# Depthwise convolution of a scan layer as stacks of three shifted rows on four column quarters of TensorE

## The chip, the cores and the metric

The kernel runs on one NeuronCore of a Trainium2 chip. The metric is the time of one execution on the device, in microseconds (us); lower is better. TensorE (PE) does matrix products and transposes, VectorE (DVE) and ScalarE (ACT) element-wise work, GpSimd (POOL) element-wise work on SBUF alone, and SyncE (SP) issues the DMAs. Matmuls write into PSUM, eight banks of 512 float32 columns on 128 partitions.

## What is computed

Two layers on eight images of 56 x 56 positions and 192 channels, all in float32. The first layer normalizes groups, makes queries, keys and values by depthwise 3 x 3 convolutions and 1 x 1 projections, attends with three heads and adds the result to its input. The second layer, in which the change lies, is a two-dimensional selective scan over 384 inner channels. Cut to its core:

```python
xz = jnp.einsum('bhwc,oc->bhwo', x, in_proj_w)
xa, z = jnp.split(xz, 2, axis=-1)
xc = conv_general_dilated(xa, conv_w, (1, 1), 'SAME', feature_group_count=Din) + conv_b
xc = silu(xc)
...
h = exp(d_l * A) * h + d_l * B_l * u_l     # scan over 3136 positions, 16 states
y = sum(h * C_l, axis=-1)
...
```

The convolution is depthwise: each of the 384 channels has its own nine weights, and no channel mixes with another.

## The kernel before

**Tiling.** The 3136 positions of an image are cut into 7 chunks of `T = 448` (`RPC = 8` rows of 56); the 384 channels into `NJ = 3` blocks of 128. A scan step is one state `n` of 16 for one chunk of one direction: 4 directions x 7 chunks x 16 states = 448 steps for an image, 3584 in all. A step takes one product of step size and B row on GpSimd (L1119), three exponentials on ScalarE (L1133) and three scans on VectorE (L1150). To multiply by C and sum the states, TensorE turns the state tile `h` (L1196), ScalarE scales it while it leaves PSUM (L1212), and TensorE turns it back into an accumulating PSUM tile `y` (L1230). For three or four of the 16 states (`BY_POOL`), GpSimd multiplies by C instead (L1248, L1252), and TensorE adds the result with the identity (L1267). Seven buffers `h` are shared by all of this, and five buffers `bb` hold the B rows that DMAs bring.

**Stages.** `front(b)` is everything for image `b` up to the convolved channels: loading, first layer, in-projection, depthwise convolution, Silu. `x_proj` makes step sizes and the rows B and C; `finish` normalizes, gates and projects. The front of image 0 runs ahead of any scan. The front of image `b + 1` runs beside the scan of image `b`; the last image's scan has only a finish beside it.

**What sets the order.** The program is recorded in an order made by hand-written planning code (`Sched`). Each piece of work is a generator that yields `(engine, cost, cells read, cells written)`; the planner keeps a clock for each engine, gives the next instruction to the stage with the earliest time less its rank, and so fixes the order in which each engine's instructions stand. On the chip, engines run their instructions in that order and wait on semaphores. The costs are formulas in the code, `t_mm(n) = n * 0.00171` for a matmul among them. Two rules matter here. `pace` lets the front spend its planned TensorE time in proportion to the scan's progress: beside a given scan step stands a given share of the front's whole TensorE cost. And `keep_busy` puts filler matmuls (L1363) where TensorE's planned clock has a gap. DMAs all go through SyncE's one queue, in planned order.

**The convolution.** In `project`, for each channel block `j`, seven in-projections (two matmuls each, L853) go to PSUM, and `xa_out` (L818) evicts each with its bias into a full-image tile `xa` in SBUF. Then, for each of the seven chunks, `conv_rows` (L452) makes nine matmuls, one for each tap: the stationary operand is a 128 x 128 diagonal matrix of that tap's weights (`dg`, loaded from `dgx_d`), the moving operand the image shifted by the tap, with the rows and columns that fall off the image left out. `xv_out` (L824) evicts the sum, and `stored` applies Silu, and writes the image out once in row order and once in column order. `xa` and `xv` have one buffer each. During scans the front has one PSUM bank at a time (`share("bank1", 1)`); in the head it has eight.

The three lines that carry the convolution:

```python
for t in TAPS:
    yield PE, t_mm(T), xa.c[max(c - 1, 0):c + 2] + dg.c, pcv.c if t == 8 else []
    conv_rows(pcv.ap[:, :T].rearrange("p (h w) -> p h w", w=HW), dg.ap[:, t], ...)
```

Of the kernel before, what the change touches and what calls it, by code (L numbers as in the profile page):

```python
# [8 lines left out]
F32 = mybir.dt.float32  # L9
AF = mybir.ActivationFunctionType  # L10
ALU = mybir.AluOpType
# [6 lines left out]
B, HW, C = 8, 56, 192  # L18
L = HW * HW
CP = 96  # L20
NB = C // CP
T = 448
RPC = T // HW
NCH = L // T
# [10 lines left out]
NJ = DIN // 128  # L35
# [18 lines left out]
PE, ACT, DVE, POOL, SP = range(5)  # L54
# [10 lines left out]
def t_mm(n):  # L65
    return n * 0.00171
# [10 lines left out]
def t_dve(n):  # L77
    return 0.07 + n * 0.00105
# [195 lines left out]
def kernel(  # L274
# [24 lines left out]
    nc = tc.nc  # L299
# [13 lines left out]
    ident = const.tile([128, 128], F32, name="ident")  # L313
# [3 lines left out]
    zeros = fill("zeros", [128, 128], 0.0)  # L317
# [60 lines left out]
    dconst = ctx.enter_context(tc.tile_pool(name="dconst", bufs=1, space=DRAM))  # L378
# [2 lines left out]

    dgq_d = dconst.tile([CP, NB, 9, CP], F32, name="dgq_d")
    dgkv_d = dconst.tile([CP, NB, 9, CP], F32, name="dgkv_d")
    dgx_d = dconst.tile([128, NJ, 9, 128], F32, name="dgx_d")
    with tc.tile_pool(name="taps", bufs=2) as taps:
        for dst, src, p, nb in ((dgq_d, dw_q, CP, NB), (dgkv_d, dw_kv, CP, NB), (dgx_d, conv_w, 128, NJ)):
            w = taps.tile([p, nb, 9], F32, name="w")
            nc.sync.dma_start(w, src.rearrange("(b p) t -> p b t", p=p))
            for bl in range(nb):
                d = taps.tile([p, 9, p], F32, name="d")  # L390
                for t in range(9):
                    nc.vector.tensor_scalar(d[:, t], ident[:p, :p], w[:, bl, t:t + 1], None, ALU.mult)
                nc.sync.dma_start(dst[:, bl], d)


    keep = ctx.enter_context(tc.tile_pool(name="keep", bufs=1))
# [9 lines left out]
    sc = Sched()  # L406
    banks = [None]

    def bank():
        return banks[0]  # L410
# [34 lines left out]
    def conv_rows(out, lhs, img, row0, rows, t):  # L445


        dy, dx = divmod(t, 3)
        lo, hi = max(row0 + dy - 1, 0), min(row0 + dy - 1 + rows, HW)
        o0, o1 = lo - (row0 + dy - 1), hi - (row0 + dy - 1)  # L450
        a, b = max(0, 1 - dx), min(HW, HW + 1 - dx)
        nc.tensor.matmul(out[:, o0:o1, a:b], lhs, img(lo, hi)[:, :, a + dx - 1:b + dx - 1],  # L452
                         start=(t == TAPS[0]), stop=(t == TAPS[-1]))
# [19 lines left out]
    def front(b):  # L473
# [307 lines left out]
        k_nb = Cell()  # L781
        with tc.tile_pool(name=f"fw_{b}", bufs=1) as fw, tc.tile_pool(name=f"fi_{b}", bufs=2) as pool:
            fi, fv = Rings(pool, 2), Rings(fw, 1)
            wx = fw.tile([CP, NB, DIN], F32, name="wx")
            wz = fw.tile([CP, NB, DIN], F32, name="wz")
            k_w = [Cell(), Cell()]
            yield from scaled_weights(wx, k_w[0], 0, rstd1, k_gn1)
            yield from scaled_weights(wz, k_w[1], 1, rstd1, k_gn1)
            pn = yield bank()
            for i, w in enumerate((wx, wz)):  # L790
                yield PE, 1.2, [k_w[i], k_gn1], pn.c if i else []
                for j in range(NJ):
# [13 lines left out]

            tiles, ends = {}, []

            def load_x1():
                for j in range(NJ):  # L810
                    for c in range(NCH):
                        xt = yield fi("xt2", [CP, NB, T])
                        yield from dma([k_x1[c]], xt.c, 5.0, xt.ap, x1d[:, :, c * T:(c + 1) * T])
                        tiles[j, c] = xt

            def xa_out(pin, xa, j, c):
                yield DVE, t_dve(T), pin.c + [k_nb], [xa.c[c]]
                nc.vector.tensor_scalar(xa.ap[:, c * RPC:(c + 1) * RPC].rearrange("p h w -> p (h w)"), pin.ap[:, :T],  # L818
                                        nbias[:, j:j + 1], None, ALU.add)
                pin.free()  # L820

            def xv_out(pcv, xv, j, c):
                yield ACT, t_act(T), pcv.c, [xv.c[c]]
                nc.scalar.activation(xv.ap[:, c * T:(c + 1) * T], pcv.ap[:, :T], AF.Identity, bias=cb[:, j])  # L824
                pcv.free()

            def stored(xv, j):
                k1 = Cell()
                yield ACT, t_act(L) + 2.6, xv.c, [k1]
                nc.scalar.activation(xv.ap, xv.ap, AF.Silu)  # L830
                nc.scalar.preload_act_table_set(EXP_LN)
                yield from dma([k1], [k_xcs[0][c][j] for c in range(NCH)], 6.6, xcs[0][:, j], xv.ap)
                for c in range(NCH):
                    xw = yield fi("xw", [128, RPC, HW])
                    yield ACT, t_act(T), [k1], xw.c
                    nc.scalar.copy(xw.ap, xv.ap.rearrange("p (h w) -> p w h", w=HW)[:, c * RPC:(c + 1) * RPC])
                    if c == NCH - 1:
                        xv.free()
                    yield from dma(xw.c, [k_xcs[1][c][j]], 3.0, xcs[1][:, j, c * T:(c + 1) * T],
                                   xw.ap.rearrange("p a b -> p (a b)"), [xw])  # L840

            def project():
                for j in range(NJ):
                    dg = yield fi("dg", [128, 9, 128], bufs=1)
                    yield from dma([], dg.c, 5.0, dg.ap, dgx_d[:, j])
                    xa = yield fv("xa", [128, HW, HW], parts=NCH)
                    for c in range(NCH):
                        yield lambda: (j, c) in tiles
                        xt = tiles[j, c]
                        pin = yield bank()  # L850
                        yield PE, 2 * t_mm(T), xt.c + [k_w[0]], pin.c
                        for bl in range(NB):
                            nc.tensor.matmul(pin.ap[:, :T], wx[:, bl, j * 128:(j + 1) * 128], xt.ap[:, bl],  # L853
                                             start=(bl == 0), stop=(bl == NB - 1))
                        xt.free()
                        sc.spawn(xa_out(pin, xa, j, c))
                    xv = yield fv("xv", [128, L], parts=NCH)
                    for c in range(NCH):
                        pcv = yield bank()
                        for t in TAPS:  # L860
                            yield PE, t_mm(T), xa.c[max(c - 1, 0):c + 2] + dg.c, pcv.c if t == 8 else []
                            conv_rows(pcv.ap[:, :T].rearrange("p (h w) -> p h w", w=HW), dg.ap[:, t],
                                      lambda lo, hi: xa.ap[:, lo:hi], c * RPC, RPC, t)
                        if c == NCH - 1:
                            xa.free()
                            dg.free()
                        sc.spawn(xv_out(pcv, xv, j, c))
                    ends.append(sc.spawn(stored(xv, j)))

            lx = sc.spawn(load_x1())  # L870
            pj = sc.spawn(project())
            yield from sc.join([lx, pj])
            yield from sc.join(ends)

    def x_proj(b, todo):
# [559 lines left out]
```

## Time and profile before

| what | value |
|---|---|
| median of three runs | 18,205.7 us (18,203.6 to 18,205.72) |
| the profiled execution | 18,215.8 us, its span 18,214.1 us |
| mean granted TensorE clock | 0.982 |
| first scan starts at | 814 us |
| scans of images 1 to 6 | about 2,200 us each |
| scan of image 7, with no front beside it | 16,360 to 18,160 us |
| DMA traffic | 2,159 MB, mean 119 GB/s, 39.7% of the DMA engines' time |

The profile comes from one execution that was profiled. Busy shares are of the whole span. A group's row gives line, engine, operation, output and inputs, shapes and count, then busy time, mean length of one in nanoseconds, and the engine's idle time just before, with what ended it. TensorE's matmuls are pipelined, so the recorded length of one is longer than the distance between two starts; a float32 matmul appears as two records, each with its own weight load (PEld). A view by windows gives the busy time of each engine in stretches of the span.

### The profile page before, as it was taken

To read this page: it belongs to the slowest core of one execution; us is meant where nothing else is said; L and a number is where in the kernel's file an instruction comes from. 1 tells how busy PE (TensorE), PEld (TensorE's weight loads), DVE (VectorE), ACT (ScalarE), POOL (GpSimd) and SP (SyncE) were. 2 spreads that over 40 slices of the span, in tenths; PEclk is the share of its full clock that TensorE was granted. 3 is DMA by queue.
4 is the path that set the end of the run, shared out by engine and by line. 5 is a ranking of instruction groups with operands and counts; after the bars stand their busy time and mean duration, and the time that the engine had idled before them with its cause. 6 is when DMAs were issued, how large, how long until landed. Compare 5 with 4: busy or idle time off the path is not lost. (4 is left out here: it accounts for less than half of the span.)

```text
span 18214.1 us, 279960 instructions
## 1 busy us (share of the span) xinstructions
PE 16706.4 (92%) x99872; PEld 11743.7 (64%) x99872; DVE 14151.5 (78%) x17811; ACT 14223.5 (78%) x25030; POOL 15560.9 (85%) x5200
## 2 busy tenths in 40 slices
PE   8799999999999999999999999999999999999998
PEld 4466666666666666666666666666666666667776
DVE  2277777788878788787887877878878788888998
ACT  2377788687877878778787887878888787888888
POOL 0288899888998889888898889988899888999998
PEclk9899999999999999999999999999999999999999
DMA  1353345433453334533344334553345433453332
GB/s 54 115 161 90 94 142 158 119 90 107 140 170 97 94 112 139 163 99 95 116 147 152 99 92 120 150 150 95 96 127 155 135 93 95 135 153 120 97 96 78
DMA packets 1363539, 2158.99 MB, mean 119 GB/s; under 512 B 176112, under 2 KB 1346016, under 8 KB 1359072
## 3 DMA queue, kind: packets, MB, share of 16 engines
q1 hardware_dynamic: 1362144, 2141.09, 39.7%
q8 instruction: 791, 12.96, 0.3%
q14 instruction: 604, 4.95, 0.1%
HBM read 1649.41 MB, written 491.21 MB: 118 GB/s over the span
## 5 line engine op out<-in xcount | busy, mean ns | idle before, releaser
L1150 DVE TENSOR_TENSOR_SCAN h<-da,newc,h 128x448 f32<-128x448 f32 x9216 | 10104.9, 1137 | 1970.7 <-ACT da L1133 1380.5
L1119 POOL TENSOR_TENSOR h<-du_s,bb 128x1344 f32<-128x1344 f32 x3584 | 10825.3, 3053 | 927.5 <-PE ht L1196 816.2
L1133 ACT ACTIVATE da<-dl_s,acoef 128x448 f32<-128x448 f32 x10752 | 6750.8, 638 | 1756.9 <-DVE h L1150 1705.7
L1212 ACT ACTIVATE g<-ht,ct_s 112x384 f32<-112x384 f32 x10864 | 5847.5, 575 | 936.1 <-PE ht L1196 771.3
L1230 PEld LDWEIGHTS y<-ident,g 112*128 112x128 f32 x32592 | 3564.4, 142 | 2902.0 <-ACT g L1212 1954.4
L1230 PE MATMUL y<-ident,g 112*128 112x112 f32 x32592 | 4799.3, 268 | 654.3 <-ACT g L1212 530.1
L1196 PE MATMUL ht<-ident,h 128*112 128x128 f32 x32592 | 4944.2, 276 | 122.5 <-ACT g L1212 46.6
L1196 PEld LDWEIGHTS ht<-ident,h 128*112 128x112 f32 x32592 | 3683.2, 135 | 482.7 <-DVE h L1150 147.3
L1150 DVE TENSOR_TENSOR_SCAN h<-da,h 128x448 f32<-128x448 f32 x1536 | 1607.5, 1078 | 459.6 <-ACT da L1133 410.9
L1248 POOL TENSOR_TENSOR yp<-h,cb 128x1344 f32<-128x1344 f32 x448 | 1366.3, 3050 | 407.6 <-PE y L1267 173.7
L1248 POOL TENSOR_TENSOR h<-h,cb 128x1344 f32<-128x1344 f32 x420 | 1281.6, 3051 | 292.0 <-issue 171.9
L1363 PE MATMUL y<-zeros 128*128 128x64 f32 x11648 | 1486.5, 271 | 0.0
L1363 PEld LDWEIGHTS y<-zeros 128*128 128x128 f32 x11648 | 1444.5, 194 | 50.2 <-issue 50.2
L920 POOL TENSOR_TENSOR v<-v,xs 128x1344 f32<-128x1344 f32 x224 | 677.3, 3043 | 824.7 <-DMA dl<-v 773.6
L1252 POOL TENSOR_TENSOR yp<-yp,h 128x1344 f32<-128x1344 f32 x420 | 1280.1, 3048 | 32.2
L452 PE MATMUL bank<-xa,dg 128*128 128x440 f32 (+2 forms) x3024 | 1237.1, 535 | 24.2 <-ACT xv L824 19.2
L1267 PE MATMUL y<-yp,ident 128*128 128x448 f32 x2688 | 1223.4, 546 | 10.7 <-POOL yp L1252 10.2
L756 PE MATMUL bank<-qT,kT 128*112 128x448 f32 x2352 | 1074.5, 573 | 138.6 <-DVE oT L719 82.9
L765 PE MATMUL bank<-pT,vt 112*128 112x448 f32 x2352 | 999.9, 543 | 12.4 <-ACT g L1212 6.6
L706 ACT ACTIVATE pT<-bank,nsh 112x448 f32<-112x448 f32 x1176 | 740.1, 632 | 207.2 <-PE bank L756 167.1
L452 PE MATMUL bank<-band,dgq 96*96 96x440 f32 (+3 forms) x2016 | 806.4, 532 | 10.7 <-ACT hq L582 7.7
L452 PEld LDWEIGHTS bank<-xa,dg 128*128 128x128 f32 x3024 | 525.8, 191 | 364.6 <-issue 289.9
(146 smaller groups left out, 11082.0 us busy)
## 6 DMA issues: line engine op xcount, KB each, us to landing
bb<-rows SPq DMA_DIRECT2D x3584, 224.0 KB, 3.4
cb<-rows SPq DMA_DIRECT2D x868, 224.0 KB, 3.7
dl<-v SPq DMA_DIRECT2D x224, 672.0 KB, 5.0
du<-v SPq DMA_DIRECT2D x224, 672.0 KB, 6.1
du_s<-du SPq DMA_DIRECT2D x224, 672.0 KB, 4.5
dl_s<-dl SPq DMA_DIRECT2D x224, 672.0 KB, 4.6
xt<-x1d SPq DMA_DIRECT2D x224, 336.0 KB, 4.6
xch<-xv SPq DMA_DIRECT2D x24, 1568.0 KB, 7.3
```

The lines of the kernel that those rows point to most:

```text
L452: nc.tensor.matmul(out[:, o0:o1, a:b], lhs, img(lo, hi)[:, :, a + dx - 1:b + dx - 1], start=(t == TAPS[0]), stop=(t == TAPS[-1]))
L756: nc.tensor.matmul(ps.ap[:TP, :T], kts[h][:, kb * TP:(kb + 1) * TP], qh.ap, start=True, stop=True)
L1119: nc.gpsimd.tensor_tensor(h.ap, du.ap, bb.ap.unsqueeze(1).to_broadcast([128, NJ, T]), ALU.mult)
L1133: nc.scalar.activation(da.ap[:, :T], dl.ap[:, j], AF.Exp, scale=acoef[:, k * NJ + j, n:n + 1])
L1150: nc.vector.tensor_tensor_scan(h.ap[:, j, rev], da.ap[:, 0:T][:, rev], h.ap[:, j, rev], news[i - 1].ap[:, j, n:n + 1] if ci else 0.0, ALU. ...
L1196: nc.tensor.transpose(ht.ap[:TP, j * 128:(j + 1) * 128], h.ap[:, j, s * TP:(s + 1) * TP], ident)
L1212: nc.scalar.activation(g.ap, ht.ap[:TP, :DIN], AF.Copy, scale=ct.ap[:, s, n:n + 1])
L1230: nc.tensor.matmul(y["t"].ap[:, j, s * TP:(s + 1) * TP], g.ap[:, j * 128:(j + 1) * 128], ident[:TP, :TP], is_transpose=True, start=(n == 0 ...
L1248: nc.gpsimd.tensor_tensor(to.ap, h.ap, cbr.ap.unsqueeze(1).to_broadcast([128, NJ, T]), ALU.mult)
L1252: nc.gpsimd.tensor_tensor(yp.ap, yp.ap, h.ap, ALU.add)
L1267: nc.tensor.matmul(y["t"].ap[:, j, :T], ident, yp.ap[:, j], start=False, stop=(y["left"][j] == 0))
L1363: nc.tensor.matmul(ybanks[:, 0, T:T + FILL], zeros, zeros[:, :FILL], start=False, stop=False)
```

## The change

The depthwise convolution of the second layer is laid out in another way. The evicted in-projection goes, with a zero column on each side, into a small tile `padded` and from there to a DRAM image `xpd` of 58 x 58 positions whose first and last rows are zeroed once at setup. For each channel block and chunk, three DMAs read it back into a tile `stack`: partitions 32 dy to 32 dy + 31 hold 32 channels of the rows shifted by `dy`, with four groups of channels side by side in the free dimension. A matmul with 96 rows then sums three vertical taps of 32 channels; its stationary operand is three diagonals of 32 x 32 on top of each other. Four such matmuls, one for each group of channels, write to output partitions 0, 32, 64 and 96 of the same bank; three of these fours, one for each horizontal shift `dx`, make the convolution of a chunk. The planner counts one `t_mm(T)` for each four. In-projection, loading of stacks and convolution become three stages of their own, where they were one loop before.

```diff
-    dgx_d = dconst.tile([128, NJ, 9, 128], F32, name="dgx_d")
+    dgx_d = dconst.tile([96, NJ, 4, 3, 32], F32, name="dgx_d")
+    xpd = [dconst.tile([128, NJ, HW + 2, HW + 2], F32, name=f"xpd{i}") for i in range(2)]
+    for t in xpd:
+        for row in (0, HW + 1):
+            nc.sync.dma_start(t[:, :, row], zeros[:, :HW + 2].unsqueeze(1).to_broadcast([128, NJ, HW + 2]))
...
+        for j in range(NJ):
+            d = taps.tile([96, 4, 3, 32], F32, name="d3")
+            for g in range(4):
+                for dx in range(3):
+                    nc.vector.tensor_scalar(d[:, g, dx], id3, w3[:, j, g, dx:dx + 1], None, ALU.mult)
+            nc.sync.dma_start(dgx_d[:, j], d)
...
-            def xa_out(pin, xa, j, c):
-                yield DVE, t_dve(T), pin.c + [k_nb], [xa.c[c]]
-                nc.vector.tensor_scalar(xa.ap[:, c * RPC:(c + 1) * RPC].rearrange("p h w -> p (h w)"), pin.ap[:, :T],
+            xp = xpd[b % 2]
+            padded = [fw.tile([128, RPC, HW + 2], F32, name=f"padded{i}") for i in range(2)]
+            rpad = Share([Tile(1) for _ in padded], [lambda t=t: t for t in padded], 2)
+            yield DVE, 0.8, [], []
+            for t in padded:
+                nc.vector.memset(t, 0.0)
+            k_xp = [[Cell() for _ in range(NCH)] for _ in range(NJ)]
+            stacks = {}
+
+            def xa_out(pin, j, c):
+                xa = yield rpad
+                yield DVE, t_dve(T), pin.c + [k_nb], xa.c
+                nc.vector.tensor_scalar(xa.ap[:, :, 1:HW + 1], pin.ap[:, :T].rearrange("p (h w) -> p h w", w=HW),
                                         nbias[:, j:j + 1], None, ALU.add)
                 pin.free()
+                yield from dma(xa.c, [k_xp[j][c]], 3.0, xp[:, j, 1 + c * RPC:1 + (c + 1) * RPC], xa.ap, [xa])
+
+            def load_stacks():
+                for j in range(NJ):
+                    for c in range(NCH):
+                        st = yield fi("stack", [96, 4, RPC * (HW + 2)], parts=3)
+                        for dy in range(3):
+                            src = xp[:, j, c * RPC + dy:(c + 1) * RPC + dy].rearrange("(g q) h w -> q g (h w)", q=32)
+                            yield from dma(k_xp[j][max(c - 1, 0):c + 2], [st.c[dy]], 3.0,
+                                           st.ap[32 * dy:32 * dy + 32], src)
+                        stacks[j, c] = st
...
+            def convolved():
+                for j in range(NJ):
+                    dg = yield fi("dg", [96, 4, 3, 32])
+                    yield from dma([], dg.c, 3.0, dg.ap, dgx_d[:, j])
                     xv = yield fv("xv", [128, L], parts=NCH)
                     for c in range(NCH):
+                        yield lambda: (j, c) in stacks
+                        st = stacks[j, c]
+                        stv = st.ap.rearrange("p g (h w) -> p g h w", w=HW + 2)
                         pcv = yield bank()
-                        for t in TAPS:
-                            yield PE, t_mm(T), xa.c[max(c - 1, 0):c + 2] + dg.c, pcv.c if t == 8 else []
-                            conv_rows(pcv.ap[:, :T].rearrange("p (h w) -> p h w", w=HW), dg.ap[:, t],
-                                      lambda lo, hi: xa.ap[:, lo:hi], c * RPC, RPC, t)
+                        for dx in range(3):
+                            yield PE, t_mm(T), st.c + dg.c, pcv.c if dx == 2 else []
+                            for g in range(4):
+                                nc.tensor.matmul(pcv.ap[32 * g:32 * g + 32, :T].rearrange("p (h w) -> p h w", w=HW),
+                                                 dg.ap[:, g, dx], stv[:, g, :, dx:dx + HW],
+                                                 start=(dx == 0), stop=(dx == 2))
+                        st.free()
                         sc.spawn(xv_out(pcv, xv, j, c))
...
-            pj = sc.spawn(project())
-            yield from sc.join([lx, pj])
+            pj = [sc.spawn(g()) for g in (project, load_stacks, convolved)]
+            yield from sc.join([lx] + pj)
```

More of the change, by code (lines that the diff above doesn't have):

```diff
@@ L383 @@
     dgkv_d = dconst.tile([CP, NB, 9, CP], F32, name="dgkv_d")
-    dgx_d = dconst.tile([128, NJ, 9, 128], F32, name="dgx_d")
+    dgx_d = dconst.tile([96, NJ, 4, 3, 32], F32, name="dgx_d")
[3 more added lines that the diff above has]
+            nc.sync.dma_start(t[:, :, row], zeros[:, :HW + 2].unsqueeze(1).to_broadcast([128, NJ, HW + 2]))
     with tc.tile_pool(name="taps", bufs=2) as taps:
-        for dst, src, p, nb in ((dgq_d, dw_q, CP, NB), (dgkv_d, dw_kv, CP, NB), (dgx_d, conv_w, 128, NJ)):
+        for dst, src, p, nb in ((dgq_d, dw_q, CP, NB), (dgkv_d, dw_kv, CP, NB)):
             w = taps.tile([p, nb, 9], F32, name="w")
@@ L393 @@
                 nc.sync.dma_start(dst[:, bl], d)
+        id3 = taps.tile([96, 32], F32, name="id3")
+        w3 = taps.tile([96, NJ, 4, 3], F32, name="w3")
+        for dy in range(3):
+            rows = slice(32 * dy, 32 * dy + 32)
+            nc.vector.tensor_copy(id3[rows], ident[rows, rows])
+            nc.sync.dma_start(w3[rows].rearrange("c j g x -> c (j g) x"),
+                              conv_w[:, 3 * dy:3 * dy + 3].rearrange("(q c) x -> c q x", c=32))
+        for j in range(NJ):
[4 more added lines that the diff above has]
+            nc.sync.dma_start(dgx_d[:, j], d)
     keep = ctx.enter_context(tc.tile_pool(name="keep", bufs=1))
@@ L814, in load_x1 @@
                         tiles[j, c] = xt
-            def xa_out(pin, xa, j, c):
-                yield DVE, t_dve(T), pin.c + [k_nb], [xa.c[c]]
-                nc.vector.tensor_scalar(xa.ap[:, c * RPC:(c + 1) * RPC].rearrange("p h w -> p (h w)"), pin.ap[:, :T],
+            xp = xpd[b % 2]
[10 more added lines that the diff above has]
+                nc.vector.tensor_scalar(xa.ap[:, :, 1:HW + 1], pin.ap[:, :T].rearrange("p (h w) -> p h w", w=HW),
                                         nbias[:, j:j + 1], None, ALU.add)
                 pin.free()
+                yield from dma(xa.c, [k_xp[j][c]], 3.0, xp[:, j, 1 + c * RPC:1 + (c + 1) * RPC], xa.ap, [xa])
[3 more added lines that the diff above has]
+                        st = yield fi("stack", [96, 4, RPC * (HW + 2)], parts=3)
+                        for dy in range(3):
+                            src = xp[:, j, c * RPC + dy:(c + 1) * RPC + dy].rearrange("(g q) h w -> q g (h w)", q=32)
+                            yield from dma(k_xp[j][max(c - 1, 0):c + 2], [st.c[dy]], 3.0,
+                                           st.ap[32 * dy:32 * dy + 32], src)
+                        stacks[j, c] = st
             def xv_out(pcv, xv, j, c):
@@ L843, in project @@
                 for j in range(NJ):
-                    dg = yield fi("dg", [128, 9, 128], bufs=1)
-                    yield from dma([], dg.c, 5.0, dg.ap, dgx_d[:, j])
-                    xa = yield fv("xa", [128, HW, HW], parts=NCH)
                     for c in range(NCH):
@@ L855, in project @@
                         xt.free()
[L856 removed]
+                        ends.append(sc.spawn(xa_out(pin, j, c)))
+            def convolved():
+                for j in range(NJ):
+                    dg = yield fi("dg", [96, 4, 3, 32])
+                    yield from dma([], dg.c, 3.0, dg.ap, dgx_d[:, j])
                     xv = yield fv("xv", [128, L], parts=NCH)
                     for c in range(NCH):
+                        yield lambda: (j, c) in stacks
+                        st = stacks[j, c]
+                        stv = st.ap.rearrange("p g (h w) -> p g h w", w=HW + 2)
                         pcv = yield bank()
[L860 to L866 removed]
+                        for dx in range(3):
[5 more added lines that the diff above has]
+                        st.free()
                         sc.spawn(xv_out(pcv, xv, j, c))
+                    dg.free()
                     ends.append(sc.spawn(stored(xv, j)))
             lx = sc.spawn(load_x1())
[L871 to L872 removed]
+            pj = [sc.spawn(g()) for g in (project, load_stacks, convolved)]
+            yield from sc.join([lx] + pj)
             yield from sc.join(ends)
```

## The prediction

> **What bounds the kernel now.** I read the page first: busy shares, then the groups.
>
> ```profile
> span 18214.1 us, 279960 instructions
> PE 16706.4 (92%) x99872; PEld 11743.7 (64%) x99872; DVE 14151.5 (78%) x17811; ACT 14223.5 (78%) x25030; POOL 15560.9 (85%) x5200
> L1119 POOL TENSOR_TENSOR h<-du_s,bb 128x1344 f32<-128x1344 f32 x3584 | 10825.3, 3053 | 927.5 <-PE ht L1196 816.2
> L1363 PE MATMUL y<-zeros 128*128 128x64 f32 x11648 | 1486.5, 271 | 0.0
> L452 PE MATMUL bank<-xa,dg 128*128 128x440 f32 (+2 forms) x3024 | 1237.1, 535 | 24.2 <-ACT xv L824 19.2
> ```
>
> No engine is full. TensorE's 92% holds 1486 us of filler (L1363), which the planner sets only where it expects a gap. GpSimd makes one 3.05 us product for each of 3584 scan steps; for images 0 to 6 there are six more such operations in 16 steps (L1248, L1252), so a step costs GpSimd 3.053 x 22/16 = 4.20 us. That is a floor. The wait that most often breaks it is for TensorE's turns (816 us).
>
> Second view: the stretches of one image's scan (the fourth), each beside a stage of the next image's front. In this order: first convolutions, attention, the stretch that the change touches (in-projection and depthwise convolution), the step-size projections. Columns as named in the first row.
>
> ```profile
> core 0: us, PE busy (x) PEld busy (x) DVE busy (x) ACT busy (x) POOL busy (x), PEclk, DMA share, GB/s
> 7747.00:8037.00 290.00, 272.43 (x1745) 197.27 (x1742) 238.19 (x311) 228.48 (x427) 266.76 (x89) 1.00 0.35 100
> 8037.00:8734.00 697.00, 635.15 (x3599) 423.40 (x3599) 567.60 (x683) 576.93 (x1064) 612.49 (x204) 0.98 0.33 94
> 8734.00:9164.00 430.00, 405.93 (x2312) 278.68 (x2313) 346.27 (x424) 344.56 (x610) 386.81 (x129) 0.99 0.41 118
> 9164.00:9729.00 565.00, 518.21 (x3265) 376.46 (x3263) 459.70 (x580) 477.15 (x789) 539.43 (x180) 0.99 0.50 155
> ```
>
> Third, the scans alone (L1150, three for a step) in the same stretches:
>
> ```profile
> 7747.00:8037.00 290.00, 209.46 (x192) 1.00 0.35 100
> 8037.00:8734.00 697.00, 469.87 (x432) 0.98 0.33 94
> 8734.00:9164.00 430.00, 313.60 (x288) 0.99 0.41 118
> 9164.00:9729.00 565.00, 366.14 (x337) 0.99 0.50 155
> ```
>
> That is 64, 144, 96 and 112 steps, at 4.53, 4.84, 4.48 and 5.04 us. The reader is to see that the convolution's stretch is already the fastest of the four, 7% above GpSimd's floor, with TensorE 94% busy. TensorE and GpSimd share the bound there; elsewhere several engines stand at 80 to 92%.
>
> Last, the head, where nothing hides the front of image 0 (timeline of TensorE; start, length):
>
> ```profile
> 515.87 3.36 PE L853 MATMUL bank<-xt,wx 96*128 96x448 f32 x4 [0.69 <-DMA xt<-x1d]
> 519.02 48.19 PE L452 MATMUL bank<-xa,dg 128*128 128x448 f32 x126
> 567.04 3.17 PE L853 MATMUL bank<-xt,wx 96*128 96x448 f32 x8
> ```
>
> Seven rows of nine taps are 63 matmuls and 126 records: a float32 matmul is two passes, each with a weight load, and a pass takes 48.19/126 = 0.382 us (0.375 us between starts in the scan). Three such blocks, and in-projections of about 24 us before each, fill 498 to 714 us; the first scan starts at 814.
>
> **What the Trainium skill says.** "TensorE: Matmul & The Clock Gate", Part 3 (Packing small matmuls): matmuls on different column groups run at once; three of 32 columns gave 2.38 times the speed. The same part, under The mechanism: matmuls start and end strictly in program order. "TensorEngine Tiling (Array Packing)", Key Properties: changing the tiling mode drains TensorE. No run here shows any of the three, since this kernel has no matmul of 32 output rows; the trace does agree with the order and shows the length of a drain: a pass is recorded for 0.535 us but the next starts after 0.375, so 0.16 us of draining.
>
> **The change part by part.**
>
> *TensorE.* For each of 168 blocks of eight rows, 9 matmuls of 128 columns go and 3 x 4 matmuls of 32 columns come, with the same 448 moving columns. Before: 18 passes x 0.375 = 6.75 us. After it is 24 passes, and their overlap is unknown:
> - full overlap of each four: 3 x 2 passes x 0.375 + 0.16 drain = 2.4 us. The planner's cost for the new code, one matmul for each four, assumes this;
> - none: 24 x 0.375 + 0.16 = 9.2 us;
> - half: the two passes of one matmul use the same quarter, so the second waits for the first; by the strict order the next quarter's first pass can start only together with that second pass. Starts then fall at 0, 1, 1, 2, 2, 3, 3, 4 passes, so four matmuls cost 4 passes, not 2. A block is 12 passes plus the last one's end, 13 x 0.375 + 0.16 = 5.0 us.
> I take half: it is what the skill's rule gives on the two-pass records of this trace. Weight loads of 32 columns could show too (190 ns for 128 columns and 163 for 96 on the lines, so about 0.11, an estimate); 24 of them are 2.6 us at worst, 0 if they hide as now.
>
> *What moves.* The front is paced by planned TensorE time, so a cheaper convolution gets fewer scan steps. From the instruction order of the built kernels, counting transposes (12 for a step that isn't GpSimd's, 336 steps of that kind for 448): in-projection and convolution stand beside 69 such steps before (92 steps of all), and 37 after (49: 24 for the in-projections, then 25 for the convolutions). The 43 freed steps go to the first convolutions (51 to 62), attention (98 to 115) and step-size projections (84 to 89). There the same front work is spread thinner, so an added step costs less than its stage's mean: at least 3.6 us (ScalarE's own 3 x 0.638 + 3 x 0.575), at most 4.85 (1552 us for 320 steps in those three stages). I take 4.0: 43 x 4.0 = 172 us (155 to 209).
>
> *The stretch itself.* Before: 92 steps x 4.48 = 412 us. After: in-projections 24 x 4.48 = 108 us. Convolutions: GpSimd's floor is 25 x 4.20 = 105 us. TensorE's own scan work in a step is 0.75 x 4 x 3 x (0.108 + 0.096), the pitches of the two turns, + 0.28 for the sums = 2.12 us, so 53 us, plus 21 blocks, over 0.94:
> - full: (53 + 50)/0.94 = 110 us; half: (53 + 105)/0.94 = 168; none: (53 + 193)/0.94 = 262.
> For one image: full 108 + 110 + 172 - 412 = -22 us; half 108 + 168 + 172 - 412 = +36 (19 to 73 with the added steps' bounds); none +130. So under half overlap TensorE does less and the kernel still loses: blocks that the planner priced at 2.3 us and packed with too few scan steps each take 5, and GpSimd, waiting for h buffers, loses time that it can't win back at 90% load. Seven images: -154, +252, +910.
>
> *Head.* Before 216 us. After, in-projection (21 x 1.5 = 32 us) and convolutions interleave: TensorE 32 + 105 = 137 us at half, plus some 13 before the first stack has landed (two passes and the eviction, a store as long as xcw's 3.2, a load as long as xt's 3.7 in the head), so 150: -66. Full: TensorE 85, but a block then moves 1.29 MB (in-projection input, store, three loads), 4.3 us at 300 GB/s (the DMA view of 490 to 720 us has slices of 313 to 390), 90 + 13: -110. None: 32 + 193 + 13 = 238: +22. The 100 us from the last convolution to the first scan stay.
>
> *Hidden edits.* 84 more DMAs for an image on SyncE, 20 MB (21 x 4 x 238 KB), 160 MB in all on 2159. The stretch's DMA share of 0.41 at 118 GB/s rises to about 0.65. Triples of stack loads wait for the store and for a stack buffer, and row loads (bb) queue behind them; five bb buffers, some 22 us of steps, cover a late triple. Today bb costs GpSimd 39 us. If this cover went, a late block (2.6 us) would pass to GpSimd directly, but those microseconds are in the sum already. Evictions (L818, L824), Silu and copies are the same in number; zeroing two padded tiles is about 1 us of VectorE per image; weights shrink from 576 to 147 KB. Setup: 36 small products for 27 large ones, four row-zeroing and three weight DMAs more: 0 to 5 us, taken as 2.
>
> **Sum.** Half: 252 - 66 + 2 = +188 us. Against the profiled execution's own 18,215.8 us (span 18,214.1) that is 18,404; that execution lies 10 us over the median of 18,205.7, so against the median about 18,395. With the bounds of the added steps (19 to 73 us an image, 133 to 511 for seven), 18,275 to 18,655.
>
> **The rivals.**
> - *Full overlap, faster.* One mechanism: the four quarters stream together, the planner's price is right, the stretch stays at GpSimd's floor. -154 - 110 + 2 = -262: 17,945. For it: the skill's 2.38 times on three. Against: two passes on one quarter and strict order. It decides from a block of under 4.0 us: there (53 + 21 x 4.0)/0.94 = 146 us makes an image lose 108 + 146 + 172 - 412 = 14 us, and seven such losses equal a head gain of some 90.
> - *No overlap, slower by much.* 910 + 22 + 2 = +934: 19,140. For it: nothing in the trace shows two passes at once. Against: the skill's measured packing.
> - *SyncE is the new wait:* overlap as in half or full, but stack triples hold bb back. A wait of 3 us at each of 147 blocks would add 440 us: about 18,385 with full overlap, 18,835 with half. For it: the triples wait for TensorE. Against: five bb buffers.
>
> **How the numbers follow.** Chances: half 0.50, full 0.24, none 0.16, SyncE 0.10. Prediction 18,395. The range of 17,900 to 18,850 holds full, nearly all of half and most of SyncE, and leaves none out. About 0.2% (36 us) can be told from no change: faster, full and a sliver of half, 0.27; within, 0.07 of half; slower 0.66. Of the likeliest alone: 18,275 to 18,655.
>
> **What would show it.** The starts of the column-tiled passes decide: pairs 0.375 us apart for half, fours together for full, single ones for none. The block's length (5.0, 2.4, 9.2 us); some 49 scan steps in the stretch at about 5.6 us each (4.4 if full); the first scan at about 750 us; GpSimd's wait for ht (816 us) up by 200 or more; its wait for bb near 40. The prediction is wrong if the blocks are half and the steps stay below 4.6 us, or if time is lost where no block stands.

## The result

The changed kernel takes 18,033.9 us at the median (18,029.0 to 18,040.9) against 18,205.7 us: a ratio of 0.9906, interval 0.9889 to 0.9923. It is 172 us faster, where 18,395 was predicted. The profiled execution has a span of 18,036.5 us. All times are of executions at the usual granted clock; one of experiment 5, 24,222 us at 0.63 of the clock, is left out (with it, its median is the 18,429 that a later expectation names).

The page of the changed kernel, the rows that answer to those shown of before:

```profile
span 18036.5 us, 286044 instructions
...
PE 16321.3 (90%) x102272; PEld 11619.9 (64%) x102272; DVE 14092.5 (78%) x17839; ACT 14185.9 (79%) x25030; POOL 15555.9 (86%) x5200
...
L1165 POOL TENSOR_TENSOR h<-du_s,bb 128x1344 f32<-128x1344 f32 x3584 | 10820.7, 3051 | 624.7 <-PE ht L1242 506.1
...
L1409 PE MATMUL y<-zeros 128*128 128x64 f32 x13040 | 1719.0, 273 | 0.0
```

TensorE is 385 us less busy although it holds 232 us more filler; GpSimd, at 86%, waits 310 us less for the turns (506 against 816). Most of TensorE's relief is not in the time. Below, a block is the convolution of one chunk for one channel block, the head is what runs before the first scan, and the stretch is the part of a scan beside the next image's in-projection and convolution. The blocks themselves, from the head (timeline of TensorE; start, length):

```profile
543.45 2.46 PE L908 MATMUL bank<-stack,dg 96*32 96x448 f32 x24 [0.85 <-DMA stack<-xpd]
...
606.50 2.46 PE L908 MATMUL bank<-stack,dg 96*32 96x448 f32 x24 [2.02 <-DMA stack<-xpd]
624.55 6.78 PE L908 MATMUL bank<-stack,dg 96*32 96x448 f32 x48 [15.59 <-DMA stack<-xpd]
...
643.42 2.46 PE L908 MATMUL bank<-stack,dg 96*32 96x448 f32 x24 [2.52 <-DMA stack<-xpd]
```

A row with x24 is one block: 24 passes in 2.46 us, where one after another they would take 9.0. The starts of the 24 records of the first of these blocks, in nanoseconds, show fours:

```
0 6 13 20 | 375 407 414 420 | 750 783 790 796 | 1125 1159 1165 1172 | 1500 1535 1541 1548 | 1876 1910 1917 1924
```

That is full overlap, the first rival: six times 0.375 us, and the last pass's end. The row at 624.55 holds two blocks in 6.78 us: after the 15.59 us without work the granted clock is 0.50 from 624 to 628 us, and the fours of the first of the two are 0.75 us apart. The last block ends at 645.9 us and the first scan starts at 746, 68 us earlier than before.

The scans of images 0 to 6 together take 15,413 us against 15,509, so 96 us less; image 7, with no front beside it, 10 less. With the head's 68 that is 174 of the 178 us between the two profiled spans. The 96 us are uneven: the scan of image 0 is 11 us longer, those of images 1 to 6 are 39, 16, 3, 16, 17 and 16 us shorter. Where the steps went, for the image shown in the prediction (its fourth), cut at each stage's first TensorE instruction; steps are scans divided by three:

| stage beside the scan | before: us, steps, us a step | after |
|---|---|---|
| finish of the image before, loading | 166, 23, 7.33 | 167, 23, 7.38 |
| first convolutions, up to attention | 361, 73, 4.93 | 412, 90, 4.57 |
| attention, up to the in-projection | 685, 146, 4.70 | 753, 166, 4.54 |
| in-projection and convolution | 418, 93, 4.47 | 254, 49, 5.15 |
| the rest | 575, 113, 5.09 | 616, 120, 5.12 |

The 44 freed steps cost 161 us elsewhere, 3.7 us each, and the stretch gives 164. For this image, which gains least of images 1 to 6, the exchange is nearly even; over the seven it pays 14 us on average. By windows, the stages of the changed kernel, and under them the scans alone:

```profile
core 0: us, PE busy (x) PEld busy (x) DVE busy (x) ACT busy (x) POOL busy (x), PEclk, DMA share, GB/s
...
7996.00:8748.00 752.00, 698.61 (x4095) 485.30 (x4094) 617.18 (x759) 639.29 (x1182) 679.18 (x226) 0.98 0.34 93
8748.00:9003.00 255.00, 225.79 (x1623) 144.90 (x1623) 185.44 (x228) 192.11 (x329) 198.15 (x66) 0.97 0.75 202
9003.00:9618.00 615.00, 564.19 (x3517) 410.18 (x3516) 495.52 (x628) 515.08 (x852) 579.46 (x194) 0.99 0.50 154
```

```profile
7996.00:8748.00 752.00, 541.64 (x497) 0.98 0.34 93
8748.00:9003.00 255.00, 164.63 (x149) 0.97 0.75 202
```

The middle row of the first fence is the stretch. No engine is full in it: TensorE 89%, GpSimd 78%, VectorE 73%; the DMA engines stand at 75%. A step costs 5.15 us there, 23% above GpSimd's floor, while before it was 4.47. In its second part (8852 to 9003 us, the convolutions) it is 5.87. The waits from 8852 to 9005 us (engine, output and line, releaser, total, times, longest) name part of it:

```profile
POOL yp L1294 <- PE y L1313: 31.1, 2, 27.6
DVE h L1196 <- ACT da L1179: 30.1, 27, 8.4
DVE yacc L1330 <- PE y L1313: 27.4, 1, 27.4
```

Once in this image, GpSimd waits 27.6 us for its one `yp` buffer and VectorE 27.4 us to evict `y`. Both wait for three sums on TensorE (L1313), which the plan placed one at a time behind pairs of blocks.

### The profile page after: what moved, and what is told of

It is laid out like the page before. It is cut to its first block, busy times and chain, and to the rows that moved or that the text cites. A ratio compares the mean times of both kernels' runs of the same rounds, so it can differ in the third digit from the quotient of the medians.

```text
span 18036.5 us, 286044 instructions
## 1 busy us (share of the span) xinstructions
PE 16321.3 (90%) x102272; PEld 11619.9 (64%) x102272; DVE 14092.5 (78%) x17839; ACT 14185.9 (79%) x25030; POOL 15555.9 (86%) x5200
## 5 line engine op out<-in xcount | busy, mean ns | idle before, releaser
L1276 PE MATMUL y<-ident,g 112*128 112x112 f32 x32592 | 4859.5, 269 | 690.0 <-ACT g L1258 545.7
L1276 PEld LDWEIGHTS y<-ident,g 112*128 112x128 f32 x32592 | 3556.6, 142 | 2835.8 <-ACT g L1258 1914.3
L1242 PE MATMUL ht<-ident,h 128*112 128x128 f32 x32592 | 4997.4, 277 | 133.2 <-DVE h L1196 68.7
L1409 PE MATMUL y<-zeros 128*128 128x64 f32 x13040 | 1719.0, 273 | 0.0
L1409 PEld LDWEIGHTS y<-zeros 128*128 128x128 f32 x13040 | 1663.4, 196 | 57.8 <-issue 57.8
L1313 PE MATMUL y<-yp,ident 128*128 128x448 f32 x2688 | 1218.2, 546 | 7.8 <-POOL yp L1294 4.6
L775 PEld LDWEIGHTS bank<-qT,kT 128*112 128x112 f32 x2352 | 364.6, 179 | 524.5 <-ACT pT L725 183.7
L999 PE MATMUL bank<-xd,dtw 128*128 128x448 f32 x1344 | 626.9, 571 | 34.6 <-DVE ct L938 9.1
```

The costliest lines, as they stand in the source:

```text
L775: nc.tensor.matmul(ps.ap[:TP, :T], kts[h][:, kb * TP:(kb + 1) * TP], qh.ap, start=True, stop=True)
L1242: nc.tensor.transpose(ht.ap[:TP, j * 128:(j + 1) * 128], h.ap[:, j, s * TP:(s + 1) * TP], ident)
L1276: nc.tensor.matmul(y["t"].ap[:, j, s * TP:(s + 1) * TP], g.ap[:, j * 128:(j + 1) * 128], ident[:TP, :TP], is_transpose=True, start=(n == 0 ...
L1313: nc.tensor.matmul(y["t"].ap[:, j, :T], ident, yp.ap[:, j], start=False, stop=(y["left"][j] == 0))
L1409: nc.tensor.matmul(ybanks[:, 0, T:T + FILL], zeros, zeros[:, :FILL], start=False, stop=False)
```

## The experiments

Scan sums below are those of images 0 to 6 in the profiled execution, beside 15,509 us before and 15,413 after.

**1. The quarters one after the other.** All three matmuls of a quarter, then the next quarter:

```diff
                         for dx in range(3):
                             yield PE, t_mm(T), st.c + dg.c, pcv.c if dx == 2 else []
-                            for g in range(4):
+                        for g in range(4):
+                            for dx in range(3):
```

> The changed kernel with the twelve matmuls of a block in another order: three for the first quarter, then three for the second, and so on; planner's price unchanged. Theory 'strict order' (a pass never starts before one that stands ahead of it, and the fours overlap only because four different quarters stand side by side): the passes of a quarter wait for one another, a block takes 21 passes, 21 x 0.375 + 0.16 = 8.0 us; by the sum of the prediction (53 + 21 x 8.0)/0.94 = 235 us for 25 steps, about +110 us an image and +80 in the head, some 18,850 us in all. Theory 'own queues' (each quarter goes on by itself, so a pass on a free quarter starts before an earlier one that waits): blocks stay near 2.5 us and the time within 0.3% of 18,034.

Measured: 18,257.6 us, ratio 1.0022 (1.0013 to 1.0032); scans 15,623, head 758. Neither length came. Two blocks in a row in the head (same columns as above):

```profile
543.86 7.92 PE L909 MATMUL bank<-stack,dg 96*32 96x448 f32 x48
...
595.15 7.92 PE L909 MATMUL bank<-stack,dg 96*32 96x448 f32 x48
```

3.96 us a block in such pairs (4.79 for a block alone), half of strict order's 8.0 and well over the 2.46 of unlimited own queues. Starts in a block that stands alone: 0, 401, 776, 782, 1152, 1183, 1528, 1559, 1565 ns and so on, two or three in each 375. In the program the six passes of the first quarter stand ahead of all others, and passes of one quarter are 375 ns apart; so at 782 ns, 6 ns after another start, a second quarter begins, while at least three of the six that stand ahead of it haven't started. So strict order of the program as written fell; a pass can start ahead of waiting ones, but here not of enough of them to fill all four quarters, which the order with the quarters side by side did. The scans lose 210 us for 147 blocks that are 1.5 us longer or more, about one for one: what a longer block costs TensorE in this stretch is paid in full.

**2. Two halves of 64 columns.** The length that the prediction had taken for a block, made real: each group's diagonals are padded with 32 zero columns, and two groups add into one half.

```diff
-                    dg = yield fi("dg", [96, 4, 3, 32])
+                    dg = yield fi("dg", [96, 4, 3, 64], bufs=1)
...
-                            for g in range(4):
-                                nc.tensor.matmul(pcv.ap[32 * g:32 * g + 32, :T].rearrange(...),
+                            for g in (0, 2, 1, 3):
+                                nc.tensor.matmul(pcv.ap[64 * (g // 2):64 * (g // 2) + 64, :T].rearrange(...),
```

> The changed kernel with each group's three diagonals padded with 32 zero columns, so that two groups share a half of 64 columns and add into it: the same twelve matmuls of 448 columns, of which two at a time can run together instead of four (weights 295 KB a channel block in one buffer instead of 147 in two). Planner's price unchanged at 2.3 us. A block then takes 12 passes or one more, 4.6 to 5.0 us: the length that the prediction took. Theory 'the sum was right, its block length wrong': the prediction's sum of half overlap, 18,395, or by the slope of the quarter-by-quarter run (209 us of scans for 147 blocks 1.6 us longer, 0.9 us a us) 18,034 + 147 x 2.3 x 0.9 = 18,340; so 18,280 to 18,420, slower than before. Rival 'the scans have slack for it': below 18,206.

Measured: 18,331.7 us, ratio 1.0062 (1.0045 to 1.0078), scans 15,691, head 773.

```profile
551.69 9.24 PE L909 MATMUL bank<-stack,dg 96*64 96x448 f32 x48
...
619.34 4.73 PE L909 MATMUL bank<-stack,dg 96*64 96x448 f32 x24
```

4.6 to 4.7 us a block, and slower than the kernel before, although TensorE still does less than the old 6.75. The sum of the prediction holds for the length it assumed, within its own range (18,275 to 18,655): given half overlap the change would have lost. So the new layout and its three stages bring no gain at half overlap; the overlap of four does.

**3. The quarter-by-quarter block at its own price.** Experiment 1 with the planner counting 4.05 us for a block.

```diff
-                            yield PE, t_mm(T), st.c + dg.c, pcv.c if dx == 2 else []
+                            yield PE, 1.76 * t_mm(T), st.c + dg.c, pcv.c if dx == 2 else []
```

> The quarter-by-quarter kernel (a block takes 4.05 us) with the planner's price for it at 1.76 t_mm for each dx, 4.05 us a block, instead of 2.3. Theory 'mismatch' (scans lose where the plan's price and the chip's time differ): most of the 209 us comes back, 18,060 to 18,130 us. Theory 'TensorE time' (the longer blocks themselves cost it, whatever the plan says): 18,220 to 18,290.

Measured: 18,258.5 us, 1.0020 (1.0010 to 1.0030), the same as at the low price. The mismatch theory fell here: telling the planner the true length won nothing. The stretch grew to 66 steps at 5.20 us.

**4. New convolution, old price.** The same line with `3 * t_mm(T)`.

> The changed kernel with the planner counting three t_mm for each four matmuls (nine for a block, as for the old nine taps), so that the stretch gets its old 92 scan steps back; the work on the chip is the same. Theory 'moved steps' (an image gains because cheaper convolutions hand scan steps to stages where a step costs less): an image's scan goes back to about 2,200 us, the head keeps its 68, 18,100 to 18,160 us. Theory 'relief on the spot' (TensorE's shorter work gains where it stands, and the new plan is no help because of the 27 us jam that it makes): the jam goes, the stretch runs at 4.2 to 4.3 us a step, 2,180 us an image, 17,980 to 18,040.

Measured: 18,313.9 us, 1.0053 (1.0038 to 1.0068); scans 15,676, head 759. Slower than before, and outside both expectations. The stretch has 91 steps again, but at 4.84 us each instead of 4.47, though a block's passes, now mostly in three pieces between other work, take under 3 us of TensorE (0.96 us recorded for a piece). What ended the idle time of TensorE's matmuls just before passes of blocks, from the first scan on:

```profile
  DMA stack<-xpd: 114.1, 19
  ACT xv L864: 30.8, 28
  ACT da L1179: 14.9, 2
```

In the changed kernel as it is, the first two rows have 38.3 us in 39 times and 3.7 us in 5, and the third is absent. In this run TensorE stops before blocks three times in nearly every image, for about 8, 3 and 7 us, mostly for a stack that hasn't landed; an image's scan is 24 us longer than before on average. That these stops are the cause, and what holds the stacks back under this plan, wasn't tested. Relief on the spot is worth nothing under it.

**5. Old convolution, new price.** The kernel before with `t_mm(T) / 3` for a tap.

> The kernel before, nine full matmuls, with the planner counting a third of t_mm for each (2.3 us for a block that takes 6.75). By the prediction's model of a block under-priced: (53 + 21 x 6.75)/0.94 = 207 us for 25 steps where 92 steps took 412: 108 + 207 + 172 - 412 = +75 us an image, +525 in all, about 18,730. Rival: the planned price hardly matters, since queues and buffers take up the difference: within 0.5% of 18,206.

Measured: 18,421.1 us, 1.0113 (1.0096 to 1.0130), scans 15,727. It costs, but 206 us and not 525: in the fourth image the stretch's 49 steps take 306 us (6.28 each) where the model said 108 + 207 = 315, and the freed steps cost 3.2 us each and not 4.0. An image loses 31 us on average instead of 75. Of the four combinations of convolution and price, only new with new beats the kernel before.

**6. The sums first.** The rank of the stage that adds `yp` on TensorE, raised above urgent front work.

```diff
-                            (back, 0.4), (summed, 0.0), (evicted, 0.71)):
+                            (back, 0.4), (summed, 0.95), (evicted, 0.71)):
```

> The changed kernel with one number changed: the rank of the stage that adds GpSimd's partial sums on TensorE (L1313) from 0.0 to 0.95, above urgent front work. Theory 'jam' (the expected gain of the scans is lost where these sums stand behind pairs of convolution blocks, and GpSimd's only yp buffer and VectorE's eviction wait 27 us for them, once an image): those waits go, 20 to 27 us an image, 17,850 to 17,900 us. Theory 'floor' (GpSimd's 4.20 us a step and the other stages hold the time, another wait takes the jam's place): 17,990 to 18,040.

Measured: 18,081.5 us, 0.9925 (0.9908 to 0.9942), not told apart from the changed kernel, and a little above both expectations. The two 27 us waits are gone, and the fourth image's stretch takes 255 us for 52 steps (4.90 each); but the seven scans take 15,412 us, as in the changed kernel, and the last image 43 us more. From 8860 to 9050 us VectorE waits 62.7 us for ScalarE's exponentials. Taking the jam away bought nothing: other waits took its place.

**7. Each stack load twice.** A second DMA with the same source and tile behind each.

> The changed kernel with each stack load issued twice (six DMAs for a block instead of three, 120 MB more), all else the same. Theory 'the DMAs bound the head, and lie hidden in the scans': the head grows by 21 x 0.71 MB at 212 to 300 GB/s, 50 to 70 us, the scans by less than 30 in all: 18,085 to 18,140. Theory 'DMAs hidden everywhere': within 20 us of 18,034. Theory 'SyncE's queue is the new wait in the stretch': more than 20 us an image too, over 18,220.

Measured: 19,476.6 us, 1.0692 (1.0676 to 1.0708), scans 16,684, head 930. SyncE's own waits in the whole run:

```profile
SPq L485 <- DMA stack<-xpd: 1779.4, 504, 8.1
```

The second load waits for the first to land in the same tile, 504 times 3.5 us, and the row loads behind it in the one queue wait too: GpSimd waits 354.9 us for B rows (L1167) where the changed kernel has 21.8, and the stretch went to 9.07 us a step. The kernel lost 1,440 us; if the doubled traffic costs the 161 us of experiment 8, the blocked queue costs some 1,280 of its 1,779 us of waiting, an estimate from these two runs.

**8. Copies beside the loads.** As many bytes read, but into a DRAM tile that nobody reads:

```diff
+                            yield from dma(k_xp[j][max(c - 1, 0):c + 2], [], 3.0, xpc[b, j, c, dy], src)
```

> The changed kernel with a copy beside each stack load, of the same rows from DRAM to a DRAM tile that nobody reads: as many bytes read again and as many DMAs as in the run that issued each load twice (whose second load had to wait for the first on the same tile, on SyncE), but no one waits for a landing of them. Theory 'the head is bound by its DMAs' (74% busy there): the head grows by 30 to 60 us, the scans by less than 100 in all: 18,070 to 18,190. Theory 'DMA traffic is hidden': within 20 us of 18,034, and then the whole 1,440 us of the doubled loads was SyncE waiting. Theory 'number of DMAs in SyncE's queue is the bound': over 18,400.

Measured: 18,194.9 us, 0.9993 (0.9985 to 1.0002): 161 us over the changed kernel, just over the first theory's range; the head 29 us longer, the scans 146 more. The stretch of the fourth image has the same 49 steps:

```profile
8825.00:9104.00 279.00, 237.62 (x1693) 152.21 (x1692) 185.27 (x228) 192.48 (x328) 204.72 (x68) 0.95 0.78 239
```

25 us longer for 15 MB more, in 63 more DMAs. Added DMA traffic isn't hidden in the squeezed stretch; whether its bytes or the number of DMAs cost this, the run doesn't separate. That fewer bytes would shorten it wasn't tried.

**9. The price between 1.2 and 1.7**, one number in the same line, and the kernel before at other prices, to see what a new plan does by itself:

> The changed kernel with the planner's price at 1.2 t_mm for each four (2.75 us a block, which takes 2.46; 1.0 gave 18,034 and 1.4 gave 17,945). Theory 'a stretch squeezed too tight, and more room helps': between the two, 17,970 to 18,010. Theory 'luck of one plan': no order between the prices, anywhere from 17,930 to 18,080.

> The changed kernel with the planner's price at 1.3 t_mm for each four. If 1.4's 17,945 lies on a slope, between 17,945 and 18,025; if it is one plan's luck, as likely above 18,025.

> The changed kernel with the planner's price at 1.4 t_mm for each four (3.2 us a block, which takes 2.46), so that the stretch gets some more scan steps. Theory 'mismatch': slower than the changed kernel by the share of the old price's loss, (3.2 - 2.46)/(6.9 - 2.46) of 280 us = 47 us, 18,080. Rival 'the stretch is squeezed too tight' (5.9 us a step in its second half): 17,950 to 18,010.

> The changed kernel with the planner's price at 1.5 t_mm for each four. If 1.4's 17,945 lies in a valley, 17,930 to 18,080; if it is one plan's luck, 18,050 to 18,150, near 1.7's.

> The changed kernel with the planner's price at 1.7 t_mm for each four (3.9 us a block, which takes 2.46; 3.0 gave 18,314). Theory 'more room helps up to a point': 17,920 to 18,080, a turn between 1.4 and 3.0. Theory 'luck of one plan': no order, 17,930 to 18,200.

> The kernel before, unchanged on the chip, with the planner's price for a tap at 1.1 t_mm. It shows how far a new plan alone moves the time when price and work still fit. Theory 'plan luck is small': within 30 us of the kernel before. Theory 'plan luck is as large as the effect of the change': more than 80 us off, either way.

> The kernel before, unchanged on the chip, with the planner's price for a tap at 0.9 t_mm (1.1 gave +58 us). Theory 'the price of the kernel before stands near its best, and the change is worth its time': 18,180 to 18,300. Theory 'plan luck': 18,000 to 18,100, as fast as the changed kernel without the change.

> The kernel before with the planner's price for a tap at 0.8 t_mm. Same theories: between 18,206 and the 18,429 that a third of the price gave, if the price stands near its best; 18,000 to 18,100 if one plan's luck is as large as the change.

| price in t_mm | changed kernel: us, ratio | price of a tap | kernel before: us, ratio |
|---|---|---|---|
| 1.0 | 18,033.9, 0.9906 | 0.8 | 18,156.5, 0.9967 |
| 1.2 | 18,025.1, 0.9900 | 0.9 | 18,259.9, 1.0024 |
| 1.3 | 18,066.3, 0.9921 | 1.0 | 18,205.7, 1 |
| 1.4 | 17,945.4, 0.9851 | 1.1 | 18,271.4, 1.0033 |
| 1.5 | 18,101.0, 0.9938 | 1/3 | 18,421.1, 1.0113 |
| 1.7 | 18,150.6, 0.9967 | | |
| 3.0 | 18,313.9, 1.0053 | | |

At 1.2, 1.3, 1.5 and 1.7 the time lies where the luck of one plan was expected, at 0.9 where a price near its best was; 1.4 lies just below both of its ranges, 0.8 and 1.1 between theirs. Intervals are about 0.0015 either way. Neighbours jump by up to 156 us in the first column and 103 in the second: that is the luck of one plan. The price 1.4 owes part of its gain to it, since no slope leads there from either side; that its time is the 17,945 of the prediction's rival is chance. Still, near the price of 1.0 the columns stay apart. From 1.0 to 1.5 the changed kernel's mean ratio is 0.990 (0.985 to 0.994); from 0.8 to 1.1 the other's is 1.001 (0.997 to 1.003). The change is worth about 1%, and a plan some 0.3% to 0.5% either way. The kernel at 1.4, 17,945.4 us (0.9836 to 0.9866), is the fastest of all and beats both.

## Why the prediction was wrong

**The step that failed** is the block of the likeliest case: "the two passes of one matmul use the same quarter, so the second waits for the first; by the strict order the next quarter's first pass can start only together with that second pass". The first half is right: passes of one quarter are 0.375 us apart. The second half, taken from the Trainium skill ("TensorE: Matmul & The Clock Gate", Part 3, The mechanism), is not what these runs show if the passes stand in the instruction stream as the program has them. Full overlap makes a block 2.46 us, not 5.0, and experiment 1 shows a pass starting ahead of earlier ones. Whether the engine reorders them or the lowering of the program does, the runs don't tell: that the fours overlap fully is measured, why the strict order doesn't hold stays open. The other place in that part, concurrent column groups, holds: 24 passes in 2.46 us instead of 9.0 is 3.7 times. The rival of full overlap had 2.4 us a block and was right in its mechanism; the choice between them was wrong.

**The sum from block to time** did better than its input. For a block of 4.7 us it gave the right side and an end within its range (experiment 2: 113 us slower by its ratio, 188 predicted for 5.0 us). Part of that is luck: in that run's fourth image the stretch took 291 us where 276 were predicted for the longer block, and the freed steps 3.4 us each where 4.0 were taken. For full overlap it gave -154 - 110 + 2 = -262; measured -172. Term by term:
- *Freed steps:* 43 counted from the order, 44 in the trace; 4.0 us each taken, 3.7 measured in that image.
- *The stretch:* 108 + 110 = 218 us predicted, 254 measured. In the in-projections 24 steps took 104 us, about as predicted; the convolutions took 150 us for 26 steps where the sum had 110 for 25. The sum had asked only whether TensorE or GpSimd is full. Neither is. The waits listed above and the cost of added DMA traffic (experiment 8), which the prediction had taken as hidden, say where time goes; which of them sets it isn't shown, as removing the longest pair of waits (experiment 6) bought nothing.
- *Net of the scans:* -22 us an image predicted, -14 measured over seven.
- *Head:* -110 predicted for full overlap (its terms give 216 - 103 = 113), -68 measured. The DMAs seem to bound the first part, as predicted, but at less than the 300 GB/s that the term took: from 513 to 606 us the DMA engines are 95% busy at 261 GB/s, and more traffic lengthens the head by 29 us. The last five blocks then take from 609 to 646 us: TensorE waits for stacks, its first block after the wait runs at a granted clock of 0.50, and the stacks had waited in SyncE's queue (below).

```profile
core 0: us, PE busy (x) PEld busy (x) DVE busy (x) ACT busy (x) POOL busy (x), PEclk, DMA share, GB/s
513.00:606.00 93.00, 74.24 (x428) 27.34 (x428) 11.62 (x17) 25.31 (x26) 0.00 (x0) 0.85 0.95 261
```

**The rival of SyncE** did not come in the scans: GpSimd's wait for B rows fell from 39.3 us to 21.8, and the row loads land in 3.5 us against 3.4. (SyncE itself waits 260 us for stack buffers on TensorE in the whole run.) In the head it came once (timeline of SyncE):

```profile
608.37 10.64 SPq L485 DMA_DIRECT2D xcw<-xw  x6
619.10 2.77 SPq L485 DMA_DIRECT2D stack<-xpd  x6
```

Six stores, each waiting for ScalarE's copy into one of two buffers, hold the queue for 10.64 us, and six stack loads stand behind them; TensorE has no block from 609.0 to 624.5 us. Experiment 7 shows what such a blocked queue costs in the scans.

**Of the signs named beforehand:** the fours in the starts, the 2.4 us block and the first scan at about 750 us point to full overlap, and came; the steps at 4.4 us did not (5.15), nor did a longer wait of GpSimd for `h` (it fell from 816 to 506 us). GpSimd's wait for B rows, expected near 40, is 22.

## What to carry to other kernels

A float32 depthwise convolution can be stacked on four column quarters at nearly four passes for one, if the four quarters stand next to each other in the program. But work taken from an engine that is not alone in bounding a stage is paid out in other currency: 4.3 us less per block over 147 blocks, 632 us of TensorE, bought 96 us in the scans. Where one queue issues all loads, ask what stands ahead of a new load in it. And where a planner fixes the order, try its prices on both kernels before crediting a change: a tenth of a price moved the kernel before by 0.3%, and the changed one by up to 0.9%.

## What the runs showed of the hardware

- Passes on four column quarters start 6 to 7 ns apart within a four; fours follow at 375 ns, as single passes do. In some blocks, as in the head's above, the first of a four leads the other three by about 32 ns.
- With two halves of 64 columns, pairs start 6 ns apart, and pairs follow at the same 375 ns.
- At a granted clock of 0.50 (513 to 519 us) a block takes 4.71 us instead of 2.46, its fours 0.75 us apart.
- Overtaking is limited: with a quarter's six passes standing together in the program, the overlap falls to two or three at a time (3.96 us a block in pairs instead of 2.46).
- Weight loads of 32 columns are recorded at 109 ns (median), as the prediction estimated, and hide: 24 of them lie within the 2.46 us.
- A change between full-width and quarter matmuls costs 0.09 us each way. From the last start on the one side to the first on the other it is 0.47 us in the median, both into the quarters (from L890, 15 times) and out of them (to L1276, 76 times), where a change between two full-width matmuls of this length (L890 to L1276, 61 times) keeps the ordinary 0.376. The prediction had taken 0.16. Rows around a pair of blocks (timeline of TensorE):

```profile
8850.77 1.68 PE L890 MATMUL bank<-xt,wx 96*128 96x448 f32 x4
8852.39 4.72 PE L908 MATMUL bank<-stack,dg 96*32 96x448 f32 x48
8857.04 0.51 PE L1276 MATMUL y<-ident,g 112*128 112x112 f32 x3
```
